# Six 16-head attention passes of a decoder: four row tiles of scores and four 32-column tiles of values at a time, in written order

## The chip, the cores and the metric

The kernel is one program on one core of one Trainium2 chip. The metric is the device time of one execution, in microseconds (us). The core has five instruction queues that run side by side and wait for each other through semaphores: TensorE (matrix products; in the profile PE for the products and PEld for loading the stationary operand), VectorE (DVE), ScalarE (ACT), GpSimd (POOL) and SyncE (SP, which here only issues DMAs). All data of this kernel is 32-bit float, except two masks in bfloat16; TensorE carries out each float product as two instructions, so a count of "x8" in the trace is four products of the program.

## The reference, cut to what matters

The activations `x` are 32 batch elements of 128 tokens with 128 features. Twelve residual layers are added to `x` one after the other. Six of them are attentions with 16 heads of 8 features, each on the layer-normed `x`, and only these are touched:

```
def attention(xn, kv):                        # L0a, L0x, L1a, L1x, L2x
    q, k, v = heads(xn @ Wq), heads(kv @ Wk), heads(kv @ Wv)    # 16 heads of 8
    p = softmax(q @ k.T / sqrt(8) [+ mask])   # over the keys
    return concat_heads(p @ v) [@ Wo + bo]
def keys(xn):                                 # L0f
    p = softmax(q @ k.T / sqrt(128))          # over the QUERIES, for each key
    z = l2_normalize(concat_heads(p.T-weighted v) @ Wo)
    return gelu(l2_normalize(z @ Wff))
```

L0a is causal, L0x, L1x and L2x take keys and values from a second input `ctx`, L1x has a mask as an input, L1a has no output projection, and L0f normalises its softmax the other way round and has two more products with unit-length normalisation and a GELU.

## The kernel before, in words

`stream` (line 1482) runs attention passes as one pipeline. `all` (line 1380) calls it twice: with L0a, L0x, L0f, L1a and L1x at the very start of the program, and with L2x later. The program's other layers (a routed feed-forward, a Hyena layer, a low-rank feed-forward, the attentions and the deep feed-forward of L3) follow and are not touched.

Within a pass the 32 elements are taken in eight groups of four. What is done for a group: `normed` (layer norm from the mean and variance kept in `self.mv`, by `rsqrt`, a chain of eleven small DVE instructions), `turned` (four transposes `xp`, copied out as `xnT`), `projected` (queries `qp`, copied out by ACT and DVE as `qTm`, which holds four copies, each with three of every four heads zeroed; keys `kp` to `kT`; values `vp`, copied to `va`). What is done for one element: `scores` (four products with 32 rows each, `sc`, of 512 columns: each row group of `kT` holds four heads, and the zeroed copies in `qTm` separate them; in the causal and the masked pass a product with a bfloat16 identity first puts the mask `drop` into the bank; then two exponentials by ACT into `PT`) and `values` (16 products `av`, one for each head). In `values` the stationary operand is `va`, 64 columns for each head: 8 columns hold the head's values, 8 ones (which give the softmax's sums), the rest zeros, so that four heads add up into the 64 partitions of one output. Two outputs lie side by side in the 128 partitions. In L0f (`keys`) the sum runs along the other axis of `PT`, and DVE takes it (`rcs`, line 1593), inverts it, and POOL scales the values into `vs`, with 32 columns for each head. After it `outputs` (transposes `tp`, division), `features` (`op`, `oT`), `closed` (output product `y`, addition to `X`, statistics for the next norm), and in L0f `closed`, `second`, `third`, `last` (two squared sums by ACT, two chains of `rsqrt`, a product, GELU).

The loop at the end of `stream` calls these for a step `t`, each with its own distance from the element that `scores` is at. That loop is not the order of execution: a planner puts each engine's instructions in order when the program is built, by priority and its own estimate of times. Another part of the program, `l3_ffn`, already uses `Ordered` (line 1347), which ties every instruction to the one written before it on its engine, DMAs excepted.

[...] `sc` takes two buffers of two banks, `av` two of one, and everything else shares two buffers of one bank (tag `b`), in turn.

Of the kernel before, what the change touches and what calls it, by code (L numbers as in the profile page):

```python
# [23 lines left out]
NB = 32  # L24
# [1334 lines left out]
class Fast(General):  # L1359
# [20 lines left out]
    def all(self):  # L1380
        with ExitStack() as es0:
            m = self.mat_at
            cuts = (0, m["L2a_in0"], m["L3x_q"], len(m))
            with self.tc.tile_pool(name="ctxT", bufs=1) as cx:
                self.some_mats(cx, *cuts[0:2])
                self.ctxT = cx.tile([128, NB * 128], F32, name="ctxT")
                with self.tc.tile_pool(name="small0", bufs=4) as self.sp:
                    for b in range(NB):
                        self.stats(self.X[:, b, :], b)
                    self.stream((("L0a", "causal"), ("L0x", "cross"), ("L0f", "keys"), ("L1a", "plain"), ("L1x", "masked")),  # L1390
                                context=True)
# [90 lines left out]
    def stream(self, stages, context=False):  # L1482

        nc, tc = self.nc, self.tc
        M = NB * len(stages)
        with ExitStack() as es:
# [10 lines left out]
            va2 = [one.tile([128, 4, 16, 64], F32, name=f"va{j}") for j in range(2)]  # L1497
            for v in va2:
                nc.gpsimd.memset(v, 0.0)
                for r in range(4):  # L1500
                    nc.gpsimd.memset(v.rearrange("p b (g r) c -> p (b g) r c", g=4)[:, :, r, 32 + 8 * r:40 + 8 * r], 1.0)
            keys = any(k == "keys" for _, k in stages)
            if keys:
                vs2 = [one.tile([128, 16, 32], F32, name=f"vs{j}") for j in range(2)]
                for v in vs2:
                    nc.gpsimd.memset(v, 0.0)
# [5 lines left out]
            def normed(g):  # L1512
                b = slice(4 * (g % 8), 4 * (g % 8) + 4)
                st = T[g // 8]
                v = wk.tile([128, 4], F32, tag="var", name="var")
# [20 lines left out]
            def projected(g):  # L1536
                st, s = T[g // 8], G[g]
                pre, cross, xnT = st["pre"], st["cross"], s["xnT"]
                kvT = self.ctxT[:, 512 * (g % 8):512 * (g % 8) + 512] if cross else xnT
                p = bank([128, 512], "qp")  # L1540
                self.mm(p, self.mat(f"{pre}_q"), xnT)

                qTm = wk.tile([128, 4, 4, 128], F32, tag="qTm", name="qTm")
                for r in range(4):
                    o = qTm[:, r].rearrange("p b q -> p (b q)")
                    m = self.sm("m4")[:, r:r + 1]
                    if r < 2:
                        if cross:
# [3 lines left out]
                    elif cross:  # L1552
                        nc.vector.tensor_scalar(o, p, m, st["qb"][:, r:r + 1], ALU.mult, ALU.add)
                    else:
                        nc.vector.tensor_scalar(o, p, m, None, ALU.mult)
                p = bank([128, 512], "kp")
                self.mm(p, self.mat(f"{pre}_k"), kvT)
                kT = wk.tile([128, 512], F32, tag="kT", name="kT")
                if cross:
                    nc.scalar.activation(kT, p, AF.Identity, bias=self.col(f"{pre}_bk"))  # L1560
                else:
                    nc.scalar.copy(kT, p)
                p = bank([128, 512], "vp")
                for j in range(4):
                    c = slice(128 * j, 128 * j + 128)
                    self.mm(p[:, c], kvT[:, c], self.mat(f"{pre}_v"))
# [3 lines left out]
                else:  # L1570
                    nc.scalar.copy(diagonal(va2[g % 2], 16, 64), p.rearrange("p (g r e) -> p g r e", g=16, r=4))
                s.update(qTm=qTm, kT=kT)

            def scores(n):
# [4 lines left out]
                drop = st.get("drop")  # L1579
                for f in range(2):  # L1580
                    sc = p2.tile([128, 2, 512], F32, tag="sc", name="sc")
                    if drop is not None:
                        for u in range(2):
                            self.mm(sc[:, u, :], self.identh[:, 0, :], drop, stop=False)
                    for u in range(2):
                        g = 32 * (2 * f + u)
                        self.mm(sc[:, u, :], s["kT"][g:g + 32, c], s["qTm"][g:g + 32, :, j, :], start=drop is None)
                    nc.scalar.activation(PT[:, 8 * f:8 * f + 8, :].rearrange("p h q -> p (h q)"),  # L1588
                                         sc.rearrange("p u k -> p (u k)"), AF.Exp, scale=scale)
                E[n] = PT  # L1590
                if st["kind"] == "keys":
                    rc = st["rc"][:, n % NB].rearrange("p g r -> p (g r)")
                    nc.vector.tensor_reduce(rc, PT, AX.X, ALU.add)
                    nc.vector.reciprocal(rc, rc)
                    nc.gpsimd.tensor_tensor(diagonal(vs2[n % 2], 4, 32),
# [1303 lines left out]
```

## Time and profile before

| what | us |
|---|---|
| median of 3 runs (6691.85 to 6724.39) | 6706.68 |
| the profiled execution | 6711.12 |
| its span | 6709.3 |
| first exponential of L0a, L0x, L0f, L1a, L1x (from the span's start) | 29.2, 250.5, 441.2, 676.0, 859.0 |
| end of the first call of `stream` | 1078.1 |
| second call: start, first exponential, end | 1760.0, 1782.4, 1970.9 |

A pass is here the time from its first exponential to that of the next pass. Times in the timeline are starts and durations; durations of PE overlap the next instruction by some tens of nanoseconds, so that costs on PE are best read as distances between starts.

### The profile page before, as it was taken

Reading aid. Unit: us, or ns where it says so; the run is one execution under the profiler, and the core shown is the slowest. Engines: PE = TensorE matmul, PEld = TensorE weight load, DVE = VectorE, ACT = ScalarE, POOL = GpSimd, SP = SyncE. Lnnn points to the kernel's source line nnn. Section 1 sums busy time; section 2 is a strip of 40 time slices with the busy share of each in tenths; the row PEclk is TensorE's granted clock in tenths of the full one; section 3 lists DMA queues with packets and bytes.
Section 4 is the critical chain, followed back from the end, with each engine's and each line's share of the span. In section 5 each row is a group of like instructions: output and inputs, shape, how many; then the busy total and the mean of one; then the engine's idle time right before and its main releaser. Section 6 shows DMA issues by size and latency. Waiting matters only on the chain.

```text
span 6709.3 us, 138109 instructions
## 1 busy us (share of the span) xinstructions
PE 5970.2 (89%) x56705; PEld 4192.1 (62%) x56705; DVE 4848.8 (72%) x11852; ACT 3304.5 (49%) x4413; POOL 3627.4 (54%) x4447
## 2 busy tenths in 40 slices
PE   8987896777786888887699999999999999999998
PEld 4554554675555666665466767667667676676665
DVE  3347433234434898985798898998988989889886
ACT  4445542111343555552356565565665656656554
POOL 0000001001101555551588888888888888888885
PEclk9998997666898999998899999999999999999999
DMA  1000003654200121220000000000000000000000
GB/s 38 1 1 1 1 1 147 227 174 121 73 29 19 49 51 44 49 51 23 33 1 1 11 8 2 1 14 5 1 14 5 1 11 8 1 2 1 1 1 14
DMA packets 243266, 207.49 MB, mean 31 GB/s; under 512 B 125650, under 2 KB 230457, under 8 KB 237502
## 3 DMA queue, kind: packets, MB, share of 16 engines
q1 hardware_dynamic: 239020, 161.73, 8.4%
q0 software_dynamic: 2304, 33.56, 1.3%
q8 instruction: 448, 7.34, 0.5%
q10 hardware_dynamic: 1298, 3.26, 0.1%
q14 instruction: 196, 1.61, 0.1%
HBM read 140.57 MB, written 57.93 MB: 30 GB/s over the span
## 4 chain that ended last, share of the span: by engine, by line
PE 65%; DVE 19%; ACT 5%; issue 4%; DMA 4%; POOL 3%; SPq 0%; POOLq 0%; DVEq 0%; ACTq 0%
PE qk L1342 8%; PE sc L1342 6%; PE sc L355 5%; PE av L1342 5%; PE av L355 5%; PE y L1342 5%; PE rT L1342 4%; PE vp L1342 3%; PE y L355 3%; DVE raw L1342 2%; PE ap L1342 2%; PE gp L1342 2%; PE fy L1342 2%; PE oTp L1342 2%; PE tp L355 2%
## 5 line engine op out<-in xcount | busy, mean ns | idle before, releaser
L1342 POOL TENSOR_TENSOR raw<-raw,rt 128x1024 f32<-128x1024 f32 x384 | 1035.0, 2709 | 37.5 <-DVE raw L1342 37.5
L1342 POOL TENSOR_TENSOR raw<-raw,ry 128x2048 f32<-128x2048 f32 x192 | 741.5, 3862 | 15.0
L1342 PE MATMUL qk<-wqkv,zs 128*128 128x512 f32 x1536 | 730.1, 598 | 6.0 <-DVE zs L1342 6.0
L1342 DVE TENSOR_TENSOR raw<-qk,tab 128x1024 f32<-128x1024 f32 x384 | 699.9, 1823 | 1.3
L1342 ACT COPY qk<-qk 128x1024 f32<-128x1024 f32 x384 | 388.7, 1012 | 398.2 <-PE qk L1342 398.2
L1342 DVE TENSOR_TENSOR rt<-qk,tab 128x1024 f32<-128x1024 f32 x384 | 499.0, 1299 | 104.0 <-POOL ry L1342 44.5
L1588 ACT ACTIVATE PT<-sc 128x1024 f32<-128x1024 f32 x384 | 380.2, 1022 | 357.7 <-PE sc L355 357.5
L1342 PE MATMUL rT<-ident,raw 128*128 128x128 f32 x3072 | 431.2, 279 | 86.0 <-DVE qkT L1342 59.1
L1342 PEld LDWEIGHTS rT<-ident,raw 128*128 128x128 f32 x3072 | 345.4, 142 | 232.7 <-issue 100.3
L1342 DVE TENSOR_REDUCE ss<-sq 128x16 f32<-128x1024 f32 x384 | 462.9, 1205 | 0.0
L1342 ACT ACTIVATE sq<-qk 128x1024 f32<-128x1024 f32 x384 | 407.9, 1062 | 74.9 <-DVE ss L1342 67.4
L1524 POOL TENSOR_TENSOR X<-X,brep 128x512 f32<-128x512 f32 x24 | 30.9, 1293 | 749.8 <-DVE brep L1478 381.5
L1342 PEld LDWEIGHTS y<-wo,oT 128*128 128x128 f32 x3072 | 372.9, 192 | 91.2 <-issue 89.4
L1342 ACT COPY va<-vp 128x1024 f32<-128x1024 f32 x192 | 194.9, 1015 | 450.3 <-PE vp L1342 450.3
L1342 PEld LDWEIGHTS sc<-qkT 64*128 64x128 f32 x6144 | 359.0, 188 | 81.8 <-issue 81.8
L355 PE MATMUL av<-PT,va 128*64 128x128 f32 x5120 | 366.4, 282 | 46.1 <-ACT PT L1588 42.8
L1342 PE MATMUL av<-va,P 128*64 128x65 f32 x12288 | 400.7, 223 | 0.0
L1342 ACT ACTIVATE P<-sc 128x1024 f32<-128x1024 f32 x384 | 372.4, 1022 | 51.6 <-PE sc L1342 50.6
L1342 PE MATMUL sc<-qkT 64*128 64x128 f32 x6144 | 395.8, 279 | 0.0
L355 PEld LDWEIGHTS av<-PT,va 128*64 128x64 f32 x5120 | 293.0, 139 | 161.0 <-ACT PT L1588 119.6
L1342 PEld LDWEIGHTS av<-va,P 128*64 128x64 f32 x12288 | 374.1, 137 | 23.8 <-issue 0.8
L1342 PEld LDWEIGHTS qk<-wqkv,zs 128*128 128x128 f32 x1536 | 264.9, 192 | 196.4 <-issue 189.2
(439 smaller groups left out, 13728.1 us busy)
## 6 DMA issues: line engine op xcount, KB each, us to landing
rows<-scr SPq DMA_DIRECT2D x32, 672.0 KB
tup<-whole SPq DMA_DIRECT2D x8, 2048.0 KB
gt<-tup SPq DMA_DIRECT2D x64, 256.0 KB
tdn<-whole SPq DMA_DIRECT2D x8, 2048.0 KB
gd<-tdn SPq DMA_DIRECT2D x128, 128.0 KB
T<-flt SPq DMA_DIRECT2D x16, 1024.0 KB
wqkv<-in_dqkv SPq DMA_DIRECT2D x6, 1536.0 KB
scr<-dots SPq DMA_DIRECT2D x128, 66.0 KB
```

What stands on the lines that cost most here:

```text
L355: self.nc.tensor.matmul(out, lhsT=lhsT, rhs=rhs, start=start, stop=stop)
L1342: self.last = call(*a, **k)
L1524: nc.gpsimd.tensor_tensor(self.X[:, b, :], self.X[:, b, :], st["brow"].unsqueeze(1).to_broadcast([128, 4, 128]), ALU.add)
L1588: nc.scalar.activation(PT[:, 8 * f:8 * f + 8, :].rearrange("p h q -> p (h q)"), sc.rearrange("p u k -> p (u k)"), AF.Exp, scale=scale)
```

## The change

`Ordered` is put around `stream`, so the loop at its end becomes the order of every engine. The loop is rewritten: at a step it calls `outputs`, then the late parts, then the early parts, then `scores(t)`, then `values(t - 1)`, in L0f `values(t - 2)`. `projected` is cut into `queries`, `keyed` and `valued`, which fall into different steps of a group, and `normed` and `turned` are called 7 and 5 steps ahead. `scores` writes all four row groups of an element one after the other, in four banks, after all four mask products. `va` has 32 columns for each head: two heads add up in 32 partitions, and four outputs lie side by side. In L0f POOL first adds the two halves of `PT` along the summed axis (`half`), DVE then reduces half as many elements, and `vs` has three buffers. In the first call the statistics of `X` are taken by `normed` for each group instead of for all 32 elements ahead of the pipeline.

```diff
-                    for b in range(NB):
-                        self.stats(self.X[:, b, :], b)
                     self.stream((("L0a", "causal"), ("L0x", "cross"), ("L0f", "keys"), ("L1a", "plain"), ("L1x", "masked")),
-                                context=True)
+                                context=True, fresh=True)
...
-        nc, tc = self.nc, self.tc
+        tc, plain = self.tc, self.nc
+        nc = self.nc = Ordered(plain, tc)
...
-            va2 = [one.tile([128, 4, 16, 64], F32, name=f"va{j}") for j in range(2)]
+            va2 = [one.tile([128, 4, 16, 32], F32, name=f"va{j}") for j in range(2)]
...
-                vs2 = [one.tile([128, 16, 32], F32, name=f"vs{j}") for j in range(2)]
+                vs3 = [one.tile([128, 16, 32], F32, name=f"vs{j}") for j in range(3)]
...
             def normed(g):
...
+                if g < 8 and fresh:
+                    for k in range(4 * g, 4 * g + 4):
+                        self.stats(self.X[:, k, :], k)
...
-            def projected(g):
+            def source(g):
+                return self.ctxT[:, 512 * (g % 8):512 * (g % 8) + 512] if T[g // 8]["cross"] else G[g]["xnT"]
+            def queries(g):
...
+            def keyed(g):
...
+            def valued(g):
...
+                    v = va2[g % 2]
+                    nc.scalar.copy(bass.AP(v.tensor, v.offset, [list(v.ap[0]), [64, 32], [48, 2], [1, 8]]),
+                                   p.rearrange("p (a r e) -> p a r e", a=32, r=2))
...
             def scores(n):
...
+                sc = [p2.tile([128, 2, 512], F32, tag="sc", name="sc") for _ in range(2)]
+                if drop is not None:
+                    for g in range(4):
+                        self.mm(sc[g // 2][:, g % 2, :], self.identh[:, 0, :], drop, stop=False)
+                for g in range(4):
+                    r = slice(32 * g, 32 * g + 32)
+                    self.mm(sc[g // 2][:, g % 2, :], s["kT"][r, c], s["qTm"][r, :, j, :], start=drop is None)
                 for f in range(2):
-                    sc = p2.tile([128, 2, 512], F32, tag="sc", name="sc")
-                    if drop is not None:
-                        for u in range(2):
-                            self.mm(sc[:, u, :], self.identh[:, 0, :], drop, stop=False)
-                    for u in range(2):
-                        g = 32 * (2 * f + u)
-                        self.mm(sc[:, u, :], s["kT"][g:g + 32, c], s["qTm"][g:g + 32, :, j, :], start=drop is None)
                     nc.scalar.activation(PT[:, 8 * f:8 * f + 8, :].rearrange("p h q -> p (h q)"),
...
-                    nc.vector.tensor_reduce(rc, PT, AX.X, ALU.add)
+                    half = wk.tile([128, 16, 64], F32, tag="half", name="half", bufs=1)
+                    for h in (slice(0, 8), slice(8, 16)):
+                        nc.gpsimd.tensor_tensor(half[:, h], PT[:, h, 0:64], PT[:, h, 64:128], ALU.add)
+                    nc.vector.tensor_reduce(rc, half, AX.X, ALU.add)
                     nc.vector.reciprocal(rc, rc)
...
             def values(n):
...
                 for f in range(2):
-                    for r in range(4):
-                        for t in range(2):
-                            h = 4 * (2 * f + t) + r
-                            self.mm(s["av"][64 * t:64 * t + 64, f, j % 2, :], va2[n // 4 % 2][:, j, h, :], PT[:, h, :],
-                                    start=r == 0, stop=r == 3)
+                    for r in range(2):
+                        for a in range(4):
+                            h = 8 * f + 2 * a + r
+                            self.mm(s["av"][32 * a:32 * a + 32, f, j % 2, :], va2[n // 4 % 2][:, j, h, :], PT[:, h, :],
+                                    start=r == 0, stop=r == 1)
...
-            for t in range(-4, M + 12):
-                for fn, at in ((last, 9), (third, 7), (second, 6), (closed, 5), (features, 4)):
-                    n = t - at
-                    if n >= 0 and n % 4 == 3 and n < M:
-                        fn(n // 4)
-                n = t - 2
+            after = ((last, 9), (third, 7), (second, 6), (closed, 5), (features, 4))
+            ahead = ((turned, 5), (queries, 3), (keyed, 2), (valued, 1), (normed, 7))
+            for t in range(-7, M + 10):
+                n = t - 3
                 if 0 <= n < M and n % 2 == 1:
                     outputs(n)
-                if 0 <= t - 1 < M:
-                    values(t - 1)
-                if 0 <= t < M:
-                    scores(t)
-                for fn, ahead in ((projected, 1), (turned, 2), (normed, 4)):
-                    n = t + ahead
-                    if 0 <= n < M and n % 4 == 0:
+                for fn, at in after:
+                    n = t - at
+                    if n % 4 == 3 and 0 <= n < M:
+                        fn(n // 4)
+                if context and -3 <= t < NB - 3 and t % 4 == 1:
+                    context_group((t + 3) // 4)
+                for fn, at in ahead:
+                    n = t + at
+                    if n % 4 == 0 and 0 <= n < M:
                         if fn is normed and n % NB == 0:
                             T[n // NB] = self.prepared(wk, bank, *stages[n // NB])
                         fn(n // 4)
-                if context and -2 <= t < NB - 2 and t % 4 == 2:
-                    context_group((t + 2) // 4)
+                if 0 <= t < M:
+                    scores(t)
+                for n in (t - 2, t - 1):
+                    if 0 <= n < M and (T[n // NB]["kind"] == "keys") == (n == t - 2):
+                        values(n)
+        self.nc = plain
```

## The prediction

> **What bounds the kernel now.** I read the page first (whole program), then the busy time of each pass, then TensorE's timeline in a masked pass, an unmasked one and L0f, then the groups and waits of L0f. The window table (columns: stretch, length, busy time and instructions of PE, PEld, DVE, ACT, POOL, clock, DMA):
>
> ```profile
> 29.20:250.50 221.30, 220.25 (x1711) 120.48 (x1712) 65.11 (x249) 101.83 (x126) 3.79 (x3) 1.00 0.02 7
> 250.50:441.20 190.70, 170.55 (x1571) 108.28 (x1571) 73.05 (x262) 95.00 (x121) 6.37 (x5) 0.96 0.01 1
> 441.20:676.00 234.80, 182.05 (x1552) 94.59 (x1551) 169.90 (x483) 127.25 (x234) 13.24 (x32) 0.82 0.00 1
> 676.00:859.00 183.00, 158.70 (x1506) 99.96 (x1507) 81.64 (x346) 101.46 (x145) 4.20 (x3) 0.97 0.01 1
> 859.00:1078.10 219.10, 216.99 (x1678) 117.38 (x1676) 57.94 (x185) 97.70 (x117) 6.42 (x5) 1.00 0.02 6
> 1782.40:1970.90 188.50, 164.59 (x1572) 105.03 (x1572) 54.60 (x178) 96.46 (x123) 11.02 (x12) 1.00 0.05 16
> ```
>
> In order L0a, L0x, L0f, L1a, L1x, L2x; together 1237.4 us, 18% of the span. The masked passes L0a and L1x are TensorE from end to end (220 of 221 us); in the unmasked ones it is busy 87 to 89%; in L0f it waits and DVE is busiest (72%), its clock down at 0.82. TensorE in a masked pass, then at one element of L0x, then in L0f:
>
> ```profile
> 863.40 1.13 PE L355 MATMUL sc<-qTm,kT 32*128 32x512 f32 x4
> 864.46 0.60 PE L355 MATMUL sc<-drop,identh 128*128 128x512 bf16 x2
> 865.00 1.13 PE L355 MATMUL sc<-qTm,kT 32*128 32x512 f32 x4
> 866.06 1.09 PE L355 MATMUL av<-PT,va 128*64 128x128 f32 x16
> ...
> 359.58 1.14 PE L355 MATMUL sc<-qTm,kT 32*128 32x512 f32 x8
> 360.66 1.12 PE L355 MATMUL qp<-xnT,mats 128*128 128x512 f32 x2
> ...
> 581.51 1.08 PE L355 MATMUL av<-PT,vs 128*32 128x128 f32 x32
> 582.52 1.14 PE L355 MATMUL sc<-qTm,kT 32*128 32x512 f32 x8
> ```
>
> From start to start, two row groups cost 1.06 us (863.40 to 864.46), four cost 1.08 (359.58 to 360.66): the unmasked passes often run four together already, the masked ones never, because mask products stand between. The 16 products of `values` cost 1.01 with 32 columns in L0f (581.51 to 582.52) and 2 x 0.95 with 64 (a half: 860.97 x32 to 862.87 gives 1.90). L0f's groups, and one DVE instruction while POOL clears `va` at the second start:
>
> ```profile
> L1593 DVE TENSOR_REDUCE rcs<-PT 128x16 f32<-128x2048 f32 x32 | 72.9, 2278 | 32.6 <-ACT PT L1588 32.6
> L1595 POOL TENSOR_TENSOR vs<-v,rcs 128x128 f32<-128x128 f32 x32 | 13.2, 414 | 298.9 <-DVE rcs L1594 238.2 <-DVE bnst L360 46.8 <-PE sc L355 11.8
> L1666 ACT ACTIVATE sq<-y 128x128 f32<-128x128 f32 x52 | 14.4, 278 | 21.6 <-PE y L355 20.4
> ...
> 1760.04 6.96 POOL L1499 MEMSET va<- 128x4096 f32 x2 [65.84 <-DVE bnst L360]
> 1764.05 2.98 DVE L1466 TENSOR_SCALAR qb<-c_small,cols 128x4 f32<-128x4 f32 x1
> ```
>
> The reduction is 31% of L0f by itself, POOL almost idle. A DVE instruction on 4 elements took 2.98 us, until POOL's clearing ended; elsewhere its like takes 0.16 to 0.23.
>
> **What the Trainium skill says.** "TensorE: Matmul & The Clock Gate", Part 3 (packing small matmuls), has small products in distinct row or column groups running at once, 3.07 times as fast for four 32-row tiles; the trace agrees in kind (four for the price of two, 32 columns for half of 64). "TensorEngine Tiling (Array Packing)", Gotcha 1, wants different row tiles in different PSUM banks; the changed `scores` has four banks, as the x8 runs have. "SBUF — State Buffer", "Who interferes with whom": one port pair is locked for a whole instruction by GpSimd or by a DVE instruction that needs it (fast `tensor_scalar`, two SBUF inputs), never by `tensor_reduce`. The 2.98 us agree.
>
> **The change part by part.** Work removed from TensorE: four row groups save 1.06 us on 64 masked elements, 68 us; 32 columns save 1.90 - 1.01 = 0.89 on 160 elements, 142 us. Whether that arrives depends on the new order, so I walk one group of four elements through it. Phases 0 to 3 are the step modulo 4; TensorE's order in them is: 0 `tp`, `y`; 1 `qp`; 2 `tp`, `kp`; 3 `op`, `xp`, `vp`; each time followed by scores (S, 1.07), then values (V, 1.02). Prices, start to start from the same timelines: `tp`, `op`, `xp` 0.55, `qp`, `kp` 1.0, `y`, `vp` 1.09; two exponentials 1.94; ACT copies `avs`, `oT`, `va`, `kT` 0.59; ACT's `qTm` 1.45 (cross) or 1.3, DVE's 1.5 and only after ACT's; handover 0.1. DVE: a norm 3.5 (twelve instructions 0.2 apart, four of 0.28), division 0.8.
>
> Unmasked cross pass, clock zero at S of phase 2. S ends 1.07, exponentials 1.18 to 3.12, V to 2.09. Phase 3: `op` needs the division of phase 2, which stands behind `qTm` and `normed` on DVE and ends at 3.3; `op` to 3.9; `vp` takes the bank that `op` leaves, so it waits for `oT` (4.0 to 4.6): 4.65 to 5.74; S to 6.81; exponentials 6.92 to 8.86. Phase 0: V 7.83, `tp` 8.38, `y` 9.47, S 10.54, exponentials to 12.59. Phase 1: V 11.56, `qp` 12.56, S 13.67, but ACT does `avs` and `qTm` first: exponentials 14.63 to 16.57. Phase 2: `kp` takes `qp`'s bank and waits for DVE's `qTm` until 16.2; to 17.2, where the next group begins. So 17.2 us a group, 138 a pass, where TensorE's own sum is 14.7. With masks each phase has 1.07 more, part of it in those waits: 20.2 a group. L0a also has `ctx` transposes (0.5) and statistics in `normed` (4 x 0.43), which makes `op` later: 21.3. L1a has no `op` and no `y`: 14.0.
>
> L0f. The halves cost POOL 1.2 to 1.3 each (128x512 `X<-X,brep`: 1293 ns), the reduction 1.2 (128x1024 `ss<-sq`: 1205 ns) and a reciprocal 0.25. Written order puts what follows behind it: phase 1's `second` is on DVE behind the reduction of phase 0, and TensorE's transposes `zp` stand in front of `qp` and S. From one pair of exponentials: second half done at 3.7, reduction and reciprocal 5.25, unit length (3.24, as at 566.73 to 569.97) 8.5, `zp` 9.15, `qp` 10.15, `qTm`, next exponentials at 11.5. Phase 0 has the same chain with `last`: unit length to 8.6, GELU 9.2, squares 10.8, table load 1.28 (two a group, as now), 12.1. Phase 2: 4.3. Phase 3: 7.8, since phase 1's reduction waits behind a norm that POOL's lock holds up, and POOL takes the next halves only after `vs`. Sum 35.7. Groups 0 and 1 have no late parts yet: 21 each (POOL and DVE take turns: halves 2.6, reduction and reciprocal 1.45, `vs` 0.41, handovers 0.2, 4.65 a step, plus the norm); group 2 has 30. 42 + 30 + 5 x 36 = 252. The late parts of the last groups fall into L1a: +30 (15, 11, 4).
>
> Small edits. Each cross pass has `prepared` in written order, TensorE waiting for DVE four times: +5, for L0x and L1x. Statistics by group take 32 x 0.43 from the front of DVE, but the first S now stands behind `turned(1)`, so behind the norm of the second group, and the weights' loads keep the DMAs busy until about 17 us: 0, with 9 us gain as the other end. Clearing half of `va`: 0, up to 3.5 gain at the second start, hidden behind the norms and the `ctx` load. The third `vs` buffer only allows the extra step of distance: 0. What follows the calls is not changed and costs nothing as long as it begins when they end; I allow 15 us either way for another placing by the planner.
>
> | pass | before | after |
> |---|---|---|
> | L0a | 221.3 | 8 x 21.3 + 5 = 175 |
> | L0x | 190.7 | 138 |
> | L0f | 234.8 | 252 |
> | L1a | 183.0 | 112 + 30 + 5 = 147 |
> | L1x | 219.1 | 162 + 9 (tail) = 171 |
> | L2x | 188.5 | 138 + 9 = 147 |
>
> 1237 - 1030 = 207 us. The profiled execution, 6711 us (its span 6709 and 2 around it), becomes 6504; it stands 4 us above the median, so 6500.
>
> **The rivals.** (B) The waits of the walk are mostly hidden and each pass takes its busiest engine's sum: unmasked 14.7 x 8 = 118, masked 152, L0a 156, L1a 105, L0f at DVE's sum of 21.6 a group, 173. With 9 us tails, 840: 6310. For it: masked passes stand at 99.5% busy now. Against: `vp`, `kp` and `zp` stand in one in-order queue. (C) POOL is slower or more contended than its row: halves of 2.5 us add 1.25 x 2 to each of 32 steps, 80 us: 6580. For it: POOL rows of 128x1024 in the deep feed-forward mean 2709 ns against 2361 elsewhere. (D) Slower: written order leaves nothing of TensorE's work beside the exponentials, so each step is a serial sum: S 1.18, exponentials 1.94, V 1.02, other parts 1.6 and a mask 1.07, 5.8 or 6.8; L0f 9.1: 96 x 5.8 + 64 x 6.8 + 32 x 9.1 = 1283 with 20 of starts 1303, so 6770. It decides once written order costs more than 207/192 = 1.08 us a step beyond the walk. Against: V(t-1) and the parts need nothing from exponentials(t). (E) No change: row and column groups save nothing because loads of weights bind. Against: the x8 and x32 rows above; 6705.
>
> **How the numbers follow.** The walk (6440 to 6550) 0.58; B, or half the way to it, 0.15; C 0.17; D 0.06; E 0.04. 6400 to 6605 holds the walk, C and the upper part of B. A change under 0.5% is about what runs of this kernel cannot tell apart. Faster 0.90, within 0.04, slower 0.06.
>
> **What the next profile would show.** `sc` as x8 in all passes and `va` products as 128*32, x32 in about 1.0 us; waits of `vp` for `oT` and of `kp` for `qTm`; unmasked passes near 138 us; L0f not shorter, TensorE's `zp` waiting for DVE `z`, DVE's reduction for POOL. Wrong if L0f falls below 200 us (the chains overlap), if unmasked passes stay above 160 (handovers cost more), or if layers outside the two calls move by over 15 us.

## The result, and the profile after

The changed kernel takes 6466.49 us (median of 4 runs, 6463.97 to 6477.12) against 6708.43 (6691.85 to 6724.39, 4 runs) before: 0.9643 times the time, 95% interval 0.9617 to 0.9668. The prediction was 6500 in a range of 6400 to 6605. The profiled execution took 6466.63 us, its span is 6464.7.

| stretch, us | before | predicted | after |
|---|---|---|---|
| start to first exponential | 29.2 | 29 | 31.5 |
| L0a | 221.4 | 175 | 164.4 |
| L0x | 190.6 | 138 | 131.8 |
| L0f | 234.8 | 252 | 260.2 |
| L1a | 183.0 | 147 | 149.3 |
| L1x | 219.9 | 171 | 149.9 |
| between the two calls | 681.2 | 681 | 683.7 |
| second call, start to first exponential | 22.3 | 22 | 23.3 |
| L2x | 188.5 | 147 | 132.2 |
| after the second call | 4738.3 | 4738 | 4738.5 |

Here L1x and L2x run to the end of their last addition to `X`, which comes 0.8 us after the last output product at 1078.1; so L1x has 219.9 and not 219.1. The six passes fall from 1238.2 to 987.8 us, by 250.4; the rest of the program gives 5.8 of that back. The windows of the changed kernel, in the order L0a, L0x, L0f, L1a, L1x, L2x, with the columns as before (stretch, length, busy time and instructions of PE, PEld, DVE, ACT, POOL, clock, DMA):

```profile
31.50:195.90 164.40, 147.82 (x1656) 82.70 (x1689) 76.62 (x291) 95.51 (x125) 2.55 (x2) 0.97 0.03 9
195.90:327.80 131.90, 120.49 (x1576) 70.10 (x1573) 72.48 (x259) 93.48 (x121) 7.62 (x6) 1.00 0.01 2
327.80:587.90 260.10, 140.57 (x1552) 78.50 (x1544) 160.03 (x495) 125.56 (x233) 92.15 (x96) 0.75 0.00 1
587.90:737.20 149.30, 125.35 (x1515) 69.44 (x1519) 86.54 (x339) 100.45 (x145) 2.53 (x2) 0.89 0.01 1
737.20:887.50 150.30, 139.71 (x1677) 78.86 (x1696) 66.48 (x233) 92.83 (x119) 8.20 (x7) 1.00 0.04 10
1594.00:1727.00 133.00, 120.29 (x1568) 70.88 (x1568) 61.76 (x216) 94.51 (x123) 7.61 (x6) 1.00 0.04 12
```

TensorE has some 72 us less to do in L0a, 50 in L0x, 77 in L1x and 44 in L2x with about as many instructions, and each of these passes is shorter by 56 to 70 us. L0f is the exception: its busiest engine, DVE, lost 10 us of work, POOL gained 79, and the pass became 25 us longer, with no engine busy for more than 62% of it.

The timeline of the changed kernel, first TensorE's two usual waits at L0x, then DVE's, POOL's and TensorE's part of one group of L0f, then an element of L1x:

```profile
250.84 1.13 PE L1342 MATMUL kp<-ctxT,mats 128*128 128x512 f32 x2 [0.67 <-DVE qTm L1342]
...
256.09 1.16 PE L1342 MATMUL vp<-mats,ctxT 128*128 128x128 f32 x8 [0.24 <-ACT oT L1342]
...
480.12 2.48 POOL L1342 TENSOR_TENSOR half<-PT 128x512 f32<-128x512 f32 x2 [7.30 <-ACT PT L1342]
482.64 1.22 DVE L1342 TENSOR_REDUCE rcs<-half 128x16 f32<-128x1024 f32 x1 [3.43 <-POOL half L1342]
486.86 1.11 PE L1342 MATMUL zp<-ident,z 128*128 128x128 f32 x4 [16.62 <-DVE z L1342]
487.77 1.91 PE L1342 MATMUL qp<-xnT,mats 128*128 128x512 f32 x2
489.61 1.53 PE L1342 MATMUL sc<-qTm,kT 32*128 32x512 f32 x8
...
805.79 1.14 PE L1342 MATMUL sc<-qTm,kT 32*128 32x512 f32 x8
806.86 1.08 PE L1342 MATMUL av<-PT,va 128*32 128x128 f32 x32
807.88 0.66 PE L1342 MATMUL tp<-ident,avs 128*128 128x128 f32 x4
```

Now the masked passes have four row groups together as well (x8; 1.07 from start to start) and the 16 products of an element take 1.02 (806.86 to 807.88), at the prices that the prediction used. `kp` waits for `qTm` and `vp` for `oT`, as in its walk. In L0f, DVE stands 3.43 us before the reduction until POOL's halves are done, and TensorE stands 16.62 us before `zp`. Behind this wait TensorE is slower: `qp` takes 1.84 us from start to start (487.77 to 489.61), where 0.96 is usual (360.66 to 361.62 in the kernel before), and the granted clock of the stretch from 487.7 to 491.5 is 0.64. The waits of this pass, summed (columns: total us, times, longest):

```profile
POOL half L1342 <- ACT PT L1342: 125.7, 14, 40.3
PEld zp L1342 <- DVE z L1342: 91.5, 6, 16.9
...
DVE rcs L1342 <- POOL half L1342: 63.4, 23, 3.4
```

Six times in the pass TensorE's queue stops for some 15 us in front of `zp`, with the projection and the scores of the next element behind it: together a third of the pass.

For the total times below: the layers of L3's deep feed-forward, which no kernel here touches, take about 562.6 us or about 602.5 us each, differently from kernel to kernel and sometimes from one execution to the next, so that the stretch after the second call runs from 4738 to 4934 us, and the ratios leave out executions over 1.5% above the fastest of their kernel. The profiles of before and after have this stretch at 4738 and 4739. The experiments are therefore read by the lengths of their passes in one profile each, which don't depend on it: L0x takes 131.8 us in ten of the kernels below. The ratios are to runs of the kernel before taken alongside (medians 6699 to 6759 us).

### The profile page after: what moved, and what is told of

The parts are those of the page before. It is cut to its first block, busy times and chain, and to the rows that moved or that the text cites. A ratio compares the mean times of both kernels' runs of the same rounds, so it can differ in the third digit from the quotient of the medians.

```text
span 6464.7 us, 137972 instructions
## 1 busy us (share of the span) xinstructions
PE 5634.8 (87%) x56460; PEld 3993.0 (62%) x56705; DVE 4862.1 (75%) x11852; ACT 3286.9 (51%) x4413; POOL 3699.6 (57%) x4504
## 4 chain that ended last, share of the span: by engine, by line
PE 51%; DVE 16%; POOL 2%; ACT 2%; issue 2%; DMA 0%; POOLq 0%; DVEq 0%; ACTq 0%
PE qk L1342 9%; PE sc L1342 6%; PE av L1342 6%; PE y L1342 5%; PE rT L1342 4%; PE vp L1342 4%; DVE raw L1342 2%; PE ap L1342 2%; PE gp L1342 2%; PE fy L1342 2%; PE oTp L1342 2%; PE y L355 2%; DVE ry L1342 2%; DVE work L2243 1%; PE tp L355 1%
## 5 line engine op out<-in xcount | busy, mean ns | idle before, releaser
L1342 ACT COPY va<-vp 128x1024 f32<-128x1024 f32 (+1 forms) x232 | 218.4, 942 | 506.6 <-PE vp L1342 505.2
L1342 PE MATMUL y<-wo,oT 128*128 128x128 f32 x3072 | 374.3, 275 | 0.8 <-DVE qkT L1342 0.8
L1342 PE MATMUL vp<-wqkv,zs 128*128 128x512 f32 x768 | 361.6, 593 | 0.0
```

The source lines that it names most:

```text
L1342: self.last = call(*a, **k)
```

## The experiments

My theory: the gain is work removed from TensorE (row groups, columns); the written order delivers it, and in L0f costs time through two chains in in-order queues. Rival: the new order is the gain, by closing the gaps that TensorE had. Two things have to be kept apart in it: the sequence and the distances in which the loop calls the parts, which the planner gets too, and `Ordered`, which makes this sequence binding. All pass lengths, from first exponential to first exponential, then what the profiled execution took after the second call:

| kernel | L0a | L0x | L0f | L1a | L1x | L2x | sum | rest |
|---|---|---|---|---|---|---|---|---|
| before | 221.4 | 190.6 | 234.8 | 183.0 | 219.9 | 188.5 | 1238.2 | 4738 |
| after | 164.4 | 131.8 | 260.2 | 149.3 | 149.9 | 132.2 | 987.8 | 4739 |
| e1 planner's order | 153.9 | 131.8 | 224.5 | 142.1 | 148.9 | 131.4 | 932.6 | 4895 |
| e2 64 columns | 178.9 | 146.2 | 262.4 | 168.6 | 173.6 | 147.2 | 1077.0 | 4885 |
| e3 pairs of row groups | 191.6 | 131.8 | 260.9 | 148.8 | 180.7 | 132.2 | 1046.0 | 4739 |
| e4 sums not folded | 164.4 | 131.8 | 236.8 | 149.0 | 149.8 | 133.1 | 965.0 | 4934 |
| e5 sums a step later | 164.7 | 131.8 | 252.0 | 150.9 | 149.8 | 132.2 | 981.5 | 4810 |
| e6 both, e4 and e5 | 164.5 | 131.8 | 224.8 | 153.0 | 149.9 | 132.2 | 956.2 | 4753 |
| e7 small edits undone | 157.6 | 131.8 | 391.2 | 148.0 | 149.9 | 133.1 | 1111.7 | 4752 |
| e8 before + 32 columns | 202.3 | 172.5 | 231.7 | 184.7 | 195.3 | 191.3 | 1177.7 | 4879 |
| e9 planner, not folded | 155.6 | 131.8 | 189.6 | 136.1 | 148.6 | 132.3 | 894.0 | 4879 |
| e10 order alone | 221.2 | 146.2 | 239.6 | 168.1 | 210.5 | 147.2 | 1132.8 | 4890 |
| e11 e6, zp a step later | 165.9 | 131.8 | 224.4 | 147.1 | 149.8 | 132.2 | 951.2 | 4924 |
| e12 e9, L2x as e4 | 155.4 | 131.8 | 196.0 | 133.4 | 149.4 | 132.3 | 898.4 | 4882 |

**e1: the written order undone, all new products kept.**

```diff
-        nc = self.nc = Ordered(plain, tc)
+        nc = plain
```

> The changed kernel with the planner's order in place of the written one; all else as changed. Theory (less work on TensorE brings the gain, written order only decides how much of it arrives): 6455, between 6430 and 6510; masked passes near 160 us each, L0f below 235 us because the planner may put late parts between the reductions. Rival (the written order brings the gain): above 6550, passes near those of the kernel before.

Measured: 6551.62 us (6547.72 to 6557.22), ratio 0.9775 (0.9759 to 0.9792). The passes take 932.6 us, 55 less than in written order. The total is where I had it for the rival (above 6550), but not for the rival's reason: the passes are nowhere near those of before. So `Ordered` isn't the gain. With the new products and the new sequence of calls it is a loss: 10.5 us in L0a, 35.7 in L0f, 7.2 in L1a, at most 1 in the others. That the total is nevertheless longer than the changed kernel's lies in the rest, 4895 against 4739.

**e2: 64 columns for each head again** (in the changed kernel).

```diff
-            va2 = [one.tile([128, 4, 16, 32], F32, name=f"va{j}") for j in range(2)]
+            va2 = [one.tile([128, 4, 16, 64], F32, name=f"va{j}") for j in range(2)]
...
-                    for r in range(2):
-                        for a in range(4):
-                            h = 8 * f + 2 * a + r
-                            self.mm(s["av"][32 * a:32 * a + 32, f, j % 2, :], va2[n // 4 % 2][:, j, h, :], PT[:, h, :],
-                                    start=r == 0, stop=r == 1)
+                    for r in range(4):
+                        for a in range(2):
+                            h = 8 * f + 4 * a + r
+                            self.mm(s["av"][64 * a:64 * a + 64, f, j % 2, :], va2[n // 4 % 2][:, j, h, :], PT[:, h, :],
+                                    start=r == 0, stop=r == 3)
```

> The changed kernel with 64 columns for each head in the values, two outputs side by side. Theory (by the walk: 0.89 us a step in masked passes, of which phase 3 hides little; about 1.65 a group in unmasked cross passes, 3 in L1a): about +100, 6567, between 6540 and 6590; L0f unchanged at 260. Rival (TensorE's sum binds everywhere): +142, 6609. Rival (columns bring nothing): 6466.

Measured: 6540.32 to 6703.39 us, ratio 0.9766 (0.9743 to 0.979). The passes are 89 us longer: L0a 14.5, L0x 14.4, L1a 19.3, L1x 23.7, L2x 15.0, L0f 2. The product price, 0.89 us x 32 = 28.5 a pass, arrives whole nowhere: a sixth (L1x) to a half of it (L0a, L0x, L2x) goes into places where TensorE waits anyway.

**e3: two row groups at a time, with masks two mask products before each pair.**

```diff
-                if drop is not None:
-                    for g in range(4):
-                        self.mm(sc[g // 2][:, g % 2, :], self.identh[:, 0, :], drop, stop=False)
-                for g in range(4):
-                    r = slice(32 * g, 32 * g + 32)
-                    self.mm(sc[g // 2][:, g % 2, :], s["kT"][r, c], s["qTm"][r, :, j, :], start=drop is None)
+                for f in range(2):
+                    if drop is not None:
+                        for g in (2 * f, 2 * f + 1):
+                            self.mm(sc[f][:, g % 2, :], self.identh[:, 0, :], drop, stop=False)
+                    for g in (2 * f, 2 * f + 1):
+                        r = slice(32 * g, 32 * g + 32)
+                        self.mm(sc[f][:, g % 2, :], s["kT"][r, c], s["qTm"][r, :, j, :], start=drop is None)
```

> The changed kernel with the mask products back between two pairs of row groups. Theory (only the masked passes L0a and L1x can change, 1.06 us an element, less the 1.2 us a group that TensorE waits there in phase 3): +48, 6515; unmasked passes and L0f unchanged within 2 us. Rival (four row groups at once are worth nothing): 6466.

Measured: 6517.39 to 6709.71 us, ratio 0.9761 (0.9687 to 0.9834). L0a 27.2 and L1x 30.8 us longer, 58 together of the 68 that the price gives; the unmasked passes are as they were, since without mask products this edit leaves their products in the same order.

**e4: the sums of L0f by DVE alone.**

```diff
-                    half = wk.tile([128, 16, 64], F32, tag="half", name="half", bufs=1)
-                    for h in (slice(0, 8), slice(8, 16)):
-                        nc.gpsimd.tensor_tensor(half[:, h], PT[:, h, 0:64], PT[:, h, 64:128], ALU.add)
-                    nc.vector.tensor_reduce(rc, half, AX.X, ALU.add)
+                    nc.vector.tensor_reduce(rc, PT, AX.X, ALU.add)
```

> The changed kernel with L0f's sums taken by VectorE alone from all 128 elements, in written order. Theory (L0f is a chain from exponentials to the reciprocal, 4.6 us without and 5.25 with the halves): L0f 235 to 245, total 6445. Rival (L0f is bound by VectorE's work): 32 x 1.08 more, L0f 295, total 6500.

Measured: 6438.06, 6439.40, 6587.98 and 6630.91 us, ratio 0.9606 (0.9583 to 0.963). L0f falls from 260.2 to 236.8: the folded sums are a loss of 23 us. They give POOL and DVE alternate turns (2.5 us of halves, then 1.2 of reduction, in place of 2.28 of reduction), and while a half runs some DVE instructions stand still. Two groups of the changed kernel in L0f, then the reduction of e4 (columns: count, busy us, mean ns, idle before):

```profile
L1342 DVE TENSOR_REDUCE rcs<-half 128x16 f32<-128x1024 f32 x32 | 39.0, 1218 | 63.4 <-POOL half L1342 63.4
...
L1342 DVE SCALAR_TENSOR_TENSOR rt<-rt,var 128x4 f32<-128x4 f32 x24 | 6.8, 282 | 0.8
...
L1342 DVE TENSOR_REDUCE rcs<-PT 128x16 f32<-128x2048 f32 x32 | 72.9, 2278 | 21.5 <-ACT PT L1342 21.5
```

On DVE the 23 us add up. With the halves its reductions take 34 us less (72.9 to 39.0), it waits 42 longer for their input (63.4 against 21.5), and small instructions of the norms take 15 more: `rt<-rt,var` has a mean of 282 ns here and of 162 in e4, since those that fall beside a half take some 1.1 us.

**e5: the sums called one step later, after the scores of the next element,** so that they don't stand in front of the norms and unit lengths of their own step.

```diff
                 E[n] = PT
+
+            def summed(n):
+                st, s, j = T[n // NB], G[n // 4], n % 4
+                PT = E[n]
                 if st["kind"] == "keys":
...
+                if 0 <= t - 1 < M:
+                    summed(t - 1)
                 for n in (t - 2, t - 1):
```

> The changed kernel with L0f's sums (halves, reduction, reciprocal, scaled values) of step t - 1 written behind the scores of step t, so that VectorE has the late parts of a step ahead of the sums that wait for the last exponentials. Nothing is left out. Theory (chain): phases 0 and 1 each lose about 4 us of the 12 that they take, L0f 260 to 205, total 6415, between 6395 and 6440. Rival (POOL and VectorE bound L0f by their work and the port lock): L0f within 10 us of 260, total 6466.

Measured: 6457.77 to 6528.93 us, ratio 0.9652 (0.9585 to 0.9719). A miss: L0f is 252.0 and not 205, which is what I had for the rival (within 10 us of 260). Waits in L0f of this kernel:

```profile
PEld zp L1342 <- DVE z L1342: 76.2, 6, 13.8
...
PEld av L1342 <- POOL vs L1342: 48.2, 22, 5.2
```

The wait of `zp` shrinks by 15 us, and a new one comes: in order, `values` of the element before the last now waits for `vs`, which POOL can only make after the later reduction.

**e6: e4 and e5 together.** (Both diffs above.)

> As the kernel with the later sums, but VectorE sums all 128 elements. With the chain gone VectorE's work should bind L0f (21.6 us a group with halves, 26 without): slower than the kernel with later sums and halves by 10 to 35 us. If the lock between POOL and VectorE costs more than the halves save, it is faster than that.

Measured: 6420.92 to 6450.20 us, ratio 0.9549 (0.9494 to 0.9605), the shortest total of this study. L0f 224.8, 27 us below e5, where I expected it above: of the two effects, POOL's turns and stopped instructions cost more than the half-size reduction saves. `zp` waits 49 us.

**e7: the small edits undone:** statistics of `X` ahead of the pipeline again, and two buffers of scaled values. With two buffers and the new distance of two steps an element's values are overwritten before its products read them, so this kernel computes something else in L0f; its other passes do the same work.

```diff
+                    for b in range(NB):
+                        self.stats(self.X[:, b, :], b)
...
-                                context=True, fresh=True)
+                                context=True)
...
-                vs3 = [one.tile([128, 16, 32], F32, name=f"vs{j}") for j in range(3)]
+                vs3 = [one.tile([128, 16, 32], F32, name=f"vs{j}") for j in range(2)]
...
```

> The changed kernel with two small edits undone: statistics of all 32 elements up front, two buffers of scaled values. The prediction's 0 for both: 6466 within 8 us; the first exponential comes at 29 to 40 us from the start. Other end: up to 14 us slower, if statistics up front delay the first group.

Measured: 6587.29 to 6649.38 us, ratio 0.9822 (0.9755 to 0.9889). Statistics up front: the first exponential 3.6 us later, L0a 6.8 shorter, so taking them by group costs 3 us. The buffers are another matter; this wait of L0f tells it:

```profile
PEld av L1342 <- POOL vs L1342: 236.1, 30, 9.8
```

With two buffers each step's products wait for that same step's scaling (30 times, 236 us), and L0f takes 391. The third buffer is not a detail but what makes the longer distance possible; what two buffers cost at the old distance of one step was not run.

**e8: the kernel before with 32 columns, and nothing else.** (The `va`, `values` and `outputs` parts of the change.)

> The kernel before (planner's order) with 32 columns for each head and four outputs side by side, nothing else. Theory: 0.89 us on 64 masked elements in full (57) and about 55 of the 85 us of the unmasked: 6595, between 6565 and 6630. Rival (columns need the new order): above 6670.

Measured: 6740.06 to 6781.18 us, ratio 1.0022 (0.9962 to 1.0083): the whole gain of its passes, 60 us, is hidden in the total by a longer rest. L0a 19, L0x 18 and L1x 25 us shorter, the others within 3: 44 in the masked passes, where I expected 57, and 14 in L0x, L1a and L2x, where I expected 55. TensorE's timeline in its L0x shows what is still missing:

```profile
303.46 1.12 PE L355 MATMUL sc<-qTm,kT 32*128 32x512 f32 x2
304.51 0.64 PE L355 MATMUL av<-PT,va 128*32 128x128 f32 x16
305.08 1.13 PE L355 MATMUL sc<-qTm,kT 32*128 32x512 f32 x6
```

The planner puts eight products of `values` (x16) between the first and the other three row groups of an element, which then cost their price twice (303.46 to 304.51 for one, and 309.58 to 310.64 for three at the next such element). It does so at 16 of 32 elements here and at 8 in the kernel before. But in e9 other products cut 8 of 32 apart in the same way, and its L0x is as short as any, so this by itself need not cost time. The larger part is a wait of the same pass, here and then in the kernel before:

```profile
PEld av L355 <- ACT PT L1590: 41.9, 44, 2.0
...
PEld av L355 <- ACT PT L1588: 31.6, 32, 2.0
```

The products of `values` wait for the exponentials of their own element 44 times, in the kernel before 32 times. The old loop calls `values(t - 1)` ahead of `scores(t)`; less work in `values` makes TensorE arrive at that wait earlier. In the changed kernel, and in e9 and e10, the waits of L0x have no such row. In L1a and L2x something else comes in, the clock. The window of L2x:

```profile
1709.47:1900.75 191.28, 165.97 (x1572) 90.49 (x1572) 54.98 (x180) 96.32 (x123) 6.95 (x7) 0.84 0.03 8
```

The granted clock is 0.84 here and 0.83 in L1a, against 1.00 and 0.97 in the kernel before. In the stretch from 1767.9 to 1775 it is 0.55, and three row groups take 2.02 us there from start to start (1767.91 to 1769.93), against 1.06 at 309.58. So e8 doesn't show what 32 columns alone bring in these two passes.

**e9: the changed kernel in the planner's order, sums by DVE alone.** (Diffs of e1 and e4.)

> The changed kernel with the planner's order in place of the written one, and the reduction of L0f by DVE alone over 128x2048, without POOL's halves. If the halves cost time under the planner as they do in written order (POOL and DVE taking turns), L0f falls from 224.5 us (planner with halves) to 200-215 and the six passes from 933 to 910-920. If they help where the order is the planner's, L0f is 232 or more and the sum 940 or more. The other five passes stay within 3 us of the planner's with halves (153.9, 131.8, 142.1, 148.9, 131.4).

Measured: 6506.48 us (6493.15 to 6511.02), ratio 0.9704 (0.9683 to 0.9725). The passes take 894.0 us, the least of all. The halves cost 35 us of L0f under the planner, more than in written order and more than I expected (10 to 24). L0x and L0f of e9 in the table of windows, and the reduction of L0f in its groups:

```profile
181.80:313.60 131.80, 126.80 (x1576) 72.52 (x1574) 73.55 (x259) 93.39 (x121) 5.05 (x4) 1.00 0.01 2
313.60:503.20 189.60, 158.47 (x1552) 83.65 (x1544) 164.28 (x482) 126.12 (x232) 13.43 (x32) 0.85 0.00 1
```

```profile
L1605 DVE TENSOR_REDUCE rcs<-PT 128x16 f32<-128x2048 f32 x32 | 72.9, 2278 | 7.7 <-ACT PT L1600 7.7
```

DVE is now busy for 87% of L0f (164.28 of 189.60), and the reduction, at the very price that the change set out to halve, waits only 7.7 us for its input. So the size of the reduction was not what made L0f long (it takes 72.9 us in the kernel before as well, with L0f at 234.8), but what stood still around it.

**e10: the written order alone:** the changed kernel with 64 columns (e2), pairs (e3) and sums by DVE alone (e4); order, statistics by group and third buffer stay.

> The written order alone: 64 columns for each head, score row groups in pairs (with masks two mask products, then two groups), the reduction by DVE alone; the order, the statistics by group and the third buffer stay. The three parts measured one at a time within the changed kernel (+89 for 64 columns, +58 for pairs, -23 without halves) add to 988 + 124 = 1112 us for the six passes, 126 less than the 1238 before. If the written order is by itself a loss, as the planner's run with the new products says (933 against 988), the sum is 1238 or more. L0a, L1x with masks: 164 + 14.5 + 27 = 206 and 150 + 24 + 31 = 205; L0x and L2x 147; L0f 237-240; L1a 168.

Measured: 6623.62, 6748.70, 6760.97 and 6786.11 us, too far apart for a ratio. The passes take 1132.8 us, 105 less than before; L0x:

```profile
253.90:400.10 146.20, 144.29 (x1570) 98.60 (x1570) 72.37 (x258) 95.17 (x120) 7.65 (x6) 1.00 0.01 2
```

The new sequence with `Ordered` takes 44 us off L0x, 41 off L2x, 15 off L1a, 9 off L1x and nothing off L0a, without a single product made cheaper: in L0x TensorE is now busy for 99% of the pass (144.29 of 146.20), no longer waits for exponentials before `values`, and all 32 elements have their four row groups together. So the rival holds a part. About 6 of the 44 us of L0x are the clock's: in every second group of the kernel before TensorE has a stretch at a lower one (0.58 from 281 to 285), and such a group takes 24.6 us where the others take 23.1. L2x, at clock 1.00 in both kernels, gains 41 without that. The chain from before over e10 and e4 to after parts the saving of 250 us:

| from, to | L0a | L0x | L0f | L1a | L1x | L2x | sum |
|---|---|---|---|---|---|---|---|
| before to e10: sequence, `Ordered`, small edits | 0 | -44 | +5 | -15 | -9 | -41 | -105 |
| e10 to e4: row groups and columns | -57 | -14 | -3 | -19 | -61 | -14 | -168 |
| e4 to after: folded sums | 0 | 0 | +23 | 0 | 0 | -1 | +23 |

The masked passes, where TensorE had no gap before, gain by the products (L0a wholly, L1x all but 9 of 70); L0x and L2x gain three quarters by the sequence. The 1112 of the expectation were 21 short because in the masked passes 64 columns and pairs together cost 57 (L0a) and 61 us (L1x), one at a time 42 and 55. What the new sequence brings under the planner with the old products was not run; with the new ones `Ordered` costs 71 us (e9 against e4).

**e11: e6, and `zp` cut from the unit length in front of it and called a step later** (the next product another step later).

```diff
-                    z = unit(s, "z1")
+                    s["z1"] = unit(s, "z1")
+            def crossed(g):
+                st, s = T[g // 8], G[g]
+                if st["kind"] == "keys":
+                    z = s["z1"]
                     p = bank([128, 4, 128], "zp")
...
-            after = ((last, 9), (third, 7), (second, 6), (closed, 5), (features, 4))
+            after = ((last, 9), (third, 8), (crossed, 7), (second, 6), (closed, 5), (features, 4))
```

> Sums one step later and by DVE alone (L0f 224.8, TensorE's zp waiting 49 us for DVE), and besides the transposes zp cut from the unit length before them and put a step later, the next product another step later. If L0f's length is TensorE standing in its queue behind zp, L0f falls to 175-195 us and the wait of zp for DVE to under 10. If DVE's own work and order set it by then, L0f stays at 215-230 and TensorE's wait only changes its name. Outside L0f and the start of L1a nothing moves by over 2 us.

Measured: 6560.48 to 6614.28 us, ratio 0.9836 (0.9793 to 0.9878). Waits in its L0f:

```profile
POOL vs L1342 <- DVE rcs L1342: 128.5, 13, 50.2
...
PEld av L1342 <- POOL vs L1342: 50.4, 18, 5.1
...
PEld zp L1342 <- DVE z L1342: 3.5, 6, 1.3
```

The wait of `zp` is gone (49 us to 3.5) and L0f is as long as it was, 224.4: taking this wait away gained nothing, because other time took its place. TensorE waits 50 us for `vs` in front of `values` (40 in e6), DVE's `z` waits 25 for ACT's `sq` (2.5 in e6), and TensorE is busy for 165.5 us where it was for 140.5, at a granted clock of 0.76 against 0.80. DVE is busy for 176 of the 224 us in both. The same instructions in e9's order take 35 us less, so what is left lies in the order; which part of it binds wasn't tried by itself.

**e12: the planner's order in the first call, the written one in the second, sums by DVE alone.** (With the diff of e4.)

```diff
-        nc = self.nc = Ordered(plain, tc)
+        nc = self.nc = plain if context else Ordered(plain, tc)
```

> The changed kernel with the planner's order in the first call, the written order in the second, and the reduction of L0f by DVE alone. Pass sum as in the planner's run without halves, 894 us (155.6, 131.8, 189.6, 136.1, 148.6, 132.3), within 5. What the six layers of the deep feed-forward take isn't touched: where they take 562.6 us each as in the changed kernel's run (4738 us from the end of the second call), the time is 6351 to 6375; where they take 602.5 (4880 to 4930), 6490 to 6550. If the planner's order ahead of them is what brings the longer ones, this run has them too; if they fall either way by chance, runs of both kinds may come.

Measured: 6499.27 us (6490.72 to 6507.73), ratio 0.9709 (0.9684 to 0.9734). Passes as expected (898.4), and a rest of 4882. So with 89 us less in the passes than the changed kernel it is 33 us longer in all. Whether the planner's order ahead of L3 brings the longer rest isn't settled: e1, e9 and e12 have it, but so do e4 and e11 in written order, and the kernel before, under the planner, has the shorter one.

## Why the prediction was right, point by point

**The sum.** Forecast: passes 1237 to 1030, and 6500; measured 1238 to 988, and 6466. The saving was 250 and not 207 us, and 5.8 came back outside (start 2.3, from the first call to L2x's first exponential 3.4, after the second call 0.2; 15 were allowed). That the stretch after the second call kept its length was luck as far as the runs show: with the 4895 us of e1 in place of 4739 the same passes would have given some 6620, outside the range.

**The walk of a group.** It was the right instrument and a little dear. An unmasked cross group takes 16.5 us (walk: 17.2), a masked one 19.1 (20.2), one of L1a 14.5 (14.0), one of L0a 20.1 (21.3). In L0x most of the difference arises before `vp`: S of phase 2 to `vp` is 4.19 us (251.90 to 256.09) and not 4.65, because the division before `op` ended sooner.

**The tails.** This is the largest wrong term. I added 9 us at the end of L1x and of L2x. But the first and the last groups of a call have neighbours missing: in L1x the groups take 16.9, 19.1 five times and 17.4, so that the pass with its tail is 149.9, less than 8 x 19.1 = 153; in L2x 132.2 against 8 x 17.0 = 136. Early parts that are no longer called (`normed`, `turned`, the projections) save what the tail costs. That, and 8 x 1.1 of the walk, is the 21 us at L1x.

**L0f.** Forecast slower than before, 252 against 235, by two chains; measured 260. A full group took 36.3 us (walk: 35.7), phase by phase in one of 35.5: 4.4 (4.3), 6.0 (7.8), 12.8 (12.1), 12.3 (11.5). The walk had no slower clock behind the long waits, where `qp` took 1.84 and not 1.0. Groups 0 and 1 took 20.0 and 20.5 (21); the third took 38.5 where I gave it 30, and that is the miss of 8: both chains are there from that group on. The halves took 1.27 us each, as their row of before promised, so rival C's premise fell, and still they were a loss (e4, e6, e9). That was in the walk, POOL and DVE taking turns, and I did not draw the conclusion from it that the fold by itself loses.

**Which chain.** The walk laid L0f's length on `zp` standing in TensorE's queue behind the unit length. e4 agrees, as the chain without halves is shorter; e5 and e11 correct it. Taking the reduction out from in front mostly handed the wait to `vs`, and when the wait of `zp` was taken away altogether L0f stayed as long. What is left is the fixed order of the whole; DVE's reductions, norms and unit lengths are the likely part of it, which no run shows.

**The late parts in L1a.** Forecast +30 (15, 11, 4), measured 25 (25.6, 27.7 and 15.2 us against 14.5: 11, 13, 1). `prepared` for L1x is the seventh group of L1a, 21.5 against 14.5: 7 us and not 5.

**Row groups and columns.** Here the right total had a wrong account. I priced the work removed at 68 and 142 us, 210, and the forecast of 207 read as if it were this work, delivered. Measured, the products bring 168 (58 and 89 when undone singly), and the new sequence 105, of which the prediction has no line of its own: it sits in the walk's 138 for an unmasked pass, of which 32 x 0.89 = 28 are columns and the other 24 a better sequence. The groups and waits that I read of the kernel before were those of L0f; the waits of L0x, where `av` stood for the exponentials 32 times, would have shown it. That a quarter of the elements had their row groups cut apart I took for "often run four together already".

**Small edits.** Statistics by group: 0 with 9 as the other end, measured a loss of 3. Clearing half of `va`: the second start is 1.0 longer, no gain. The third buffer: "only allows" the extra step, which is right; without it, at the new distance, L0f is 131 us longer (e7, which computes something else there).

**The rivals.** B (840 us of passes) was not reached in written order; the planner with the same products and sequence and no fold comes nearest, 894. D's serial sum fell at the first unmasked group: 16.5 us against 23.2. E fell at the x8 and x32 rows.

## What to carry to other kernels

Walk one group of an in-order pipeline through its engines with start-to-start prices from the trace; it gave each unmasked and masked group within 6% and foretold the one pass that got slower, where the busiest engine's sum (rival B's total, 6310) missed by 156 us. Where a change brings cheaper instructions and a new order, look for the waits that the order removes in the old trace, stage by stage, and test the sequence of calls, the binding order and the instructions apart: here a stage without gaps (L0a) gained by the instructions alone, one with gaps (L0x) mostly by the sequence, and binding the order cost 71 us. A long wait in front of an in-order queue is a candidate, not a cause, until an edit that removes it also shortens the stage.

## What was not expected of the hardware

**One layer, two lengths.** A layer of the deep feed-forward takes 562.6 or 562.7 us from the second one on in the profiles of before, after, e3, e6 and e7, and 601 to 603 in most layers of e1, e4, e9 and e11; e8 passes from one to the other (562.7, 594.7, 602.5, 602.7), and no profile shows the way back. Its instructions and their order are the same. The page has the same group in both, first the changed kernel, then e9:

```profile
L1342 DVE TENSOR_TENSOR rt<-qk,tab 128x1024 f32<-128x1024 f32 x384 | 499.1, 1300 | 103.9 <-POOL ry L1342 44.4
```

```profile
L1342 DVE TENSOR_TENSOR rt<-qk,tab 128x1024 f32<-128x1024 f32 x384 | 666.1, 1735 | 158.2 <-ACT qk L1342 128.0
```

The same 384 instructions take 167 us more, while DVE's small `ry<-ssv` has a median of 181 ns in e9 and 2280 in the changed kernel: in each kind another instruction of DVE is the long one. The Trainium skill, "SBUF — State Buffer", "Who interferes with whom", has the port pair that DVE shares with POOL locked for a whole instruction, and these durations agree with it. That such a layer can settle in two stable rhythms, 40 us apart, is what the runs add; that the lock makes them is not shown, and what decides between them stays open.

**Small instructions beside a half.** In the changed kernel's L0f a DVE instruction on 128x4 elements took 1.13 us at 457.09, where 0.16 is usual; it began 0.18 us after a POOL half (456.91, of 1.27) and ended with it. Under the planner (e1) the halves hold up other instructions: the norm's `xn<-X` has a mean of 772 ns, against 346 in e9. Here, folding a reduction onto POOL paid for these waits too.
